# First attention of a two-layer block: value products in runs of three units, and a written TensorE order

## The chip, the cores and the metric

The kernel runs on one core of a Trainium2 chip. A core has TensorE (PE; its weight loads are listed as PEld), VectorE (DVE), ScalarE (ACT), GpSimd (POOL) and SyncE (SP), each with its own instruction queue, and 16 DMA engines that they share. The metric is device time of one launch in microseconds (us). Before the change it was 1098.98 us, the median of 3 runs (1098.36 to 1101.94).

## The reference

Two layers work on x of shape 4 x 1024 x 256 (batch, tokens, channels), all in float32. In each layer x is normalised and shifted, an attention is added to it with a gate, it is normalised again, and a mixture of experts is added with a gate. What matters here is the first layer:

```python
Q = (hidden_states @ Wq.T).reshape(b, t, h, d)            # h = 16 heads of d = 16
latent_k = hidden_states @ Wk_down.T                      # latent width l = 64
latent_v = hidden_states @ Wv_down.T
q_lat = jnp.einsum('bthd,hdl->bthl', Q, q_to_latent)
logits = jnp.einsum('bthl,bsl->bhts', q_lat, latent_k) / math.sqrt(l)
logits = jnp.where(causal[None, None], logits, jnp.float32(-1e+30))
attn = jax.nn.softmax(logits, axis=-1)
ctx_lat = jnp.einsum('bhts,bsl->bhtl', attn, latent_v)
heads = jnp.einsum('bhtl,hld->bthd', ctx_lat, v_up)
out = heads.reshape(b, t, h * d) @ Wout.T
```

Behind it each token goes to the 2 best of 16 experts, each of them two 256 x 256 products with a layer norm and a gelu in between. The second layer has a linear attention and a mixture of 8 experts with one choice.

## The kernel before

**Attention.** The 256 channels are two groups g of 8 heads, and the heads of a group are two sets o of four. For a batch b, a group g and a set o, the causal 1024 x 1024 logits of four heads are cut into nine *units* u (the table `UNITS`): each fills 512 columns for each of the four heads, some of them in two parts so that the causal triangle leaves no column empty. There are 4 x 2 x 2 x 9 = 144 units. `scores` (L388) makes one: for each head a product with a contraction over 32 rows, the four in four row groups of the array, into two PSUM tiles `ps_s` of two banks each (the pool `ps_s` has three). ACT takes the exponential of each half into `pT` (L396), and in the units that hold a piece of the diagonal POOL clears what lies above it (L399). The value products (`sums`, L453) take `pT` as the moving operand and 32 columns of `v` as the weights, the four heads in four column groups of the array, and add up over the units into one bank `ps_av` (the pool `ps_o` has one). Units 0, 1 and 2 end the first half of the queries and units 3 to 8 the second, and then `finish` turns and divides the sums on DVE (L411 to L416).

**Work in between.** The tasks in `k.around.tasks` are generators, cut into pieces by their `yield`. `prepare(b, g)` makes the next group's queries and keys: for g = 0 four transposing pieces (`ps_lnT`, L153) and four value projections (`ps_v`, L349), and for both g four query and key projections (`ps_qk`, L364). `project(b)` is the output projection, four pieces `ps_out` (L427). `experts0.rows(b)` normalises and routes the batch for the experts (`ps_lnT` L1057, `ps_route` L794, `ps_logits` L802), and `experts0.sort(hf)` ranks the tokens of batches 0 and 1 (hf = 0) or 2 and 3 (hf = 1) by expert (`ps_rank` L895, `ps_expert` L949, `ps_gain` L1138). All of them take their PSUM tiles from `misc`, an object of the class `Spread`; in this stage that is the one bank of `ps_m`.

**Riders.** At the end of `sort(hf)` a second kind of generator, `send`, is put on `k.around.riders`. Each of its 32 steps issues one scatter from POOL (L964, an indirect DMA of 128 rows) into the buffer `sorted`, from which the expert stage loads its tiles `xs` (L1008, on SP); a POOL load `hs<-rows_in` (L1165) goes ahead of each four, with three buffers. Each scatter is made to wait for the newest logits or expert product when it was written (`paced`, L964 and `k.anchor`). `Around.step(pieces, rides)` takes so many pieces and so many rider steps.

**The loop.** For unit n the loop adds the value products of all units up to n - 2, then makes the logits of n, then takes one piece of the tasks (two at every fourth unit of batches 1 and 2) and one rider step. At the end come the remaining value products, and one piece and two rider steps at a time until the last `project` is done.

**What sets the order.** POOL's instructions stand as the program writes them (`manual_schedule(engines={Pool})`); the order on PE, DVE, ACT and SP is that of a scheduler, which may put a piece in the middle of a unit's logits. Behind the attention come the experts (`Experts0.run`): `arrive` transposes four tiles of sorted rows (`ps_xT`, L1224), `hidden` is the first product (`ps_h`, L1247) and its statistics on DVE, `output` the second product (`ps_y`, L1312), while `rows(3)` and `sort(1)` run in between; the second half of the tiles waits for `sort(1)`'s 32 scatters.

Of the kernel before, what the change touches and what calls it, by code (L numbers as in the profile page):

```python
# [33 lines left out]
class Around:  # L34
# [9 lines left out]
    def step(self, pieces=1, rides=1):  # L44
        pieces -= self.over
        while pieces > 0 and self.tasks:
            done = next(self.tasks[0], None)
            if done is None:
                self.tasks.pop(0)
            else:  # L50
                pieces -= done
        self.over = max(-pieces, 0)
        for _ in range(rides):
            if self.riders and next(self.riders[0], self) is self:
                self.riders.pop(0)

    def finish_tasks(self):
        while self.tasks:
            self.step(rides=0)
# [191 lines left out]
def attention0(ctx, k, a, after_batch=lambda b: None):  # L251
# [23 lines left out]
    class Spread:  # L275


        early, turn = True, 0

        def tile(self, shape, dtype, tag=None, name=None):  # L280
            self.turn += 1
            if self.early and self.turn % 4:
                full = ps_s.tile([P, 2, 512], dtype, tag="s", name=name)[:, 0, :]
            else:
                full = ps_m.tile([P, 512], dtype, tag="m", name=name)
            size = 1
            for n in shape[1:]:
                size *= n
            full = full[: shape[0], :size]
            if len(shape) == 2:  # L290
                return full
            names = "abc"[: len(shape) - 1]
            return full.rearrange(
                f"p ({' '.join(names)}) -> p {' '.join(names)}", **dict(zip(names, shape[1:]))
            )

    misc = Spread()
# [43 lines left out]
    def prepare(b, g):  # L341

        if g == 0:
            yield from layer_norm_steps(k, b, hT, 0, misc, "m")
            for t in range(0, NT, 2):
                ps = misc.tile([P, 2, C], F32, name="ps_v")
                for i in range(2):
                    for cc in range(CC):
                        nc.tensor.matmul(  # L349
                            ps[:, i, :], lhsT=hT[:, cc, (t + i) * P : (t + i + 1) * P],  # L350
                            rhs=wv[:, cc, :], start=cc == 0, stop=cc == CC - 1,
                        )
                nc.scalar.copy(
                    vs[b % 2][:, t : t + 2, :, :D], ps.rearrange("p t (h d) -> p t h d", d=D)
                )
                yield 1
        else:
            gates[b] = spread_rows(k, work, 0, GATE, 0, "gate_a0", b, 1)[:, 0]
        qT, *kTs = qs[g]
        for w in (wq, wk):  # L360
            for hf in range(2):
                ps = misc.tile([P, 512], F32, name="ps_qk")
                for cc in range(CC):
                    nc.tensor.matmul(  # L364
                        ps, lhsT=w[:, cc, g * P : (g + 1) * P],
                        rhs=hT[:, cc, hf * 512 : (hf + 1) * 512],
                        start=cc == 0, stop=cc == CC - 1,
                    )
                cols = slice(hf * 512, (hf + 1) * 512)
                if w is wq:  # L370
                    nc.vector.tensor_copy(qT[:, cols], ps)  # L371
                else:
                    for o in range(2):
                        nc.vector.tensor_scalar(  # L374
                            kTs[o][:, cols], ps, par[:, o : o + 1], None, ALU.mult
                        )
                yield 1
        ready[b, g] = qT, kTs

    def scores(b, g, o, u):  # L380

        qT, kTs = ready[b, g]
        pair = [ps_s.tile([P, 2, 512], F32, tag="s", name="ps_s") for _ in range(2)]
        for kb, qc, c0, w, _ in UNITS[u]:
            q1 = (qc + 1) * 512
            for hh in range(4):
                rows = slice(32 * hh, 32 * hh + 32)
                k.anchor = nc.tensor.matmul(  # L388
                    pair[hh // 2][:, hh % 2, c0 : c0 + w],
                    lhsT=kTs[o][rows, kb * P : (kb + 1) * P], rhs=qT[rows, q1 - w : q1],  # L390
                    start=True, stop=True,
                ).ins
        pTs = []
        for ps in pair:
            pT = work.tile([P, 2, 512], F32, tag="pT", name="pT", bufs=7)
            nc.scalar.activation(pT, ps, AF.Exp, scale=1.0 / L**0.5)  # L396
            for _, _, c0, _, diagonal in UNITS[u]:
                if diagonal:
                    nc.gpsimd.affine_select(  # L399
                        out=pT[:, :, c0 : c0 + P], in_=pT[:, :, c0 : c0 + P],  # L400
                        compare_op=ALU.is_ge, fill=0.0, base=0,
                        pattern=[[0, 2], [1, P]], channel_multiplier=-1,
                    )
            pTs.append(pT)
        return pTs
# [33 lines left out]
    around = k.around.tasks  # L439

    def sums():

        for b in range(B):
            on = ons[b % 2]
            for g in range(2):
                for o in range(2):
                    for qc, pieces in enumerate(SUMS):
                        po = ps_o.tile([P, 512], F32, tag="o", name="ps_av")
                        for n, (u, i) in enumerate(pieces):
                            yield place[b, g, o, u]  # L450
                            kb, _, c0, w, _ = UNITS[u][i]
                            for hh in range(4):
                                nc.tensor.matmul(  # L453
                                    po[32 * hh : 32 * hh + 32, 512 - w :],
                                    lhsT=vs[b % 2][:, kb, 8 * g + 2 * hh + o, :],
                                    rhs=exps[b, g, o, u][hh // 2][:, hh % 2, c0 : c0 + w],
                                    start=n == 0, stop=n == len(pieces) - 1,
                                )
                        finish(b, g, o, qc, po, on)
            projects.append(project(b, on))  # L460
            around.append(projects[-1])
            after_batch(b)
# [3 lines left out]
    k.around.finish_tasks()  # L466
    setup_mod(k, 1, misc, mod)
    misc.early = False
    with k.tc.manual_schedule(engines={mybir.EngineType.Pool}):
        summing = sums()  # L470
        wanted = next(summing)
        for n, (b, g, o, u) in enumerate(units):
            if n == 8:
                k.clear_rows()
            if (o, u) == (0, 0):
                while (b, g) not in ready:
                    k.around.step(rides=0)
                coming = (b, 1) if g == 0 else (b + 1, 0)
                if coming[0] < B:
                    around.insert(0, prepare(*coming))  # L480
            while wanted is not None and wanted <= n - 2:
                wanted = next(summing, None)
            exps[b, g, o, u] = scores(b, g, o, u)
            k.around.step(2 if b in (1, 2) and n % 4 == 3 else 1)
        misc.early = True
        for _ in summing:
            pass
        while projects[-1] in around:
            k.around.step(rides=2)
# [1528 lines left out]
def two_layers(ctx: ExitStack, tc: tile.TileContext, a: dict, out: bass.AP):  # L2018
# [89 lines left out]

    load_x(0)
    again = stages(attention0, attention1, True)  # L2110


# [74 lines left out]
```

## Time and profile before

| what | value |
|---|---|
| time, median of 3 runs | 1098.98 us (1098.36 to 1101.94) |
| the profiled execution | 1087.63 us, of it 1085.8 us span from first to last instruction |
| PE busy, of the span | 945.7 us (87%) |
| ACT, DVE, POOL busy | 602.5, 620.4, 336.0 us |
| attention units, 45 to 507 us of the span | PE busy 451.81 us of the 467 us from 45 to 512 |
| logits L388, values L453, PE busy | 178.8 and 165.2 us |
| exponentials L396 on ACT | 288, 1022 ns each |
| scatters L964 on POOL | 96, 1002 ns each |

The page lists busy times by engine, the span in 40 slices, the chain of work that ended last, the groups of instructions, and DMA. A matmul of float32 shows as two records, so a unit's logits of four products are eight records, or sixteen where the unit has two parts. Line numbers are those of the kernel before; after the change the same code stands 9 to 27 lines lower.

### The profile page before, as it was taken

Reading aid. Unit: us, or ns where it says so; the run is one execution under the profiler, and the core shown is the slowest. Engines: PE = TensorE matmul, PEld = TensorE weight load, DVE = VectorE, ACT = ScalarE, POOL = GpSimd, SP = SyncE. Lnnn points to the kernel's source line nnn. Section 1 sums busy time; section 2 is a strip of 40 time slices with the busy share of each in tenths; the row PEclk is TensorE's granted clock in tenths of the full one; section 3 lists DMA queues with packets and bytes.
Section 4 is the critical chain, followed back from the end, with each engine's and each line's share of the span. In section 5 each row is a group of like instructions: output and inputs, shape, how many; then the busy total and the mean of one; then the engine's idle time right before and its main releaser. Section 6 shows DMA issues by size and latency. Waiting matters only on the chain.

```text
span 1085.8 us, 18090 instructions
## 1 busy us (share of the span) xinstructions
PE 945.7 (87%) x6072; PEld 559.8 (52%) x6072; DVE 620.4 (57%) x1987; ACT 602.5 (55%) x959; POOL 336.0 (31%) x528
## 2 busy tenths in 40 slices
PE   4899999999999999889679989986997989858760
PEld 2434434443443434335568878874464656547550
DVE  5822235422465155413676767993899968564572
ACT  0368655765477555775555657766654745523430
POOL 2013211311232234663004615612550100553632
PEclk9999999999999999999899999998999899989875
DMA  6995000100010001552825556624223201458764
GB/s 206 358 346 179 1 1 6 40 1 1 1 64 1 1 30 54 201 215 78 317 88 170 197 177 189 196 75 144 67 65 148 88 2 39 141 170 264 240 205 130
DMA packets 97142, 132.89 MB, mean 122 GB/s; under 512 B 8536, under 2 KB 84216, under 8 KB 96528
## 3 DMA queue, kind: packets, MB, share of 16 engines
q1 hardware_dynamic: 84656, 97.27, 26.9%
q0 software_dynamic: 11776, 33.57, 9.9%
q8 instruction: 52, 0.85, 0.3%
q10 hardware_dynamic: 608, 0.79, 0.3%
q14 instruction: 50, 0.41, 0.1%
HBM read 67.85 MB, written 63.75 MB: 121 GB/s over the span
## 4 chain that ended last, share of the span: by engine, by line
PE 63%; DVE 19%; issue 5%; DMA 5%; ACT 4%; POOL 1%; SPq 1%; DVEq 0%; ACTq 0%; POOLq 0%
PE ps_s L388 13%; PE ps_av L453 12%; PE ps_qk L364 6%; PE ps_y L1312 5%; PE ps_h L1247 4%; PE ps_v L349 3%; PE ps_out L427 3%; PE ps_pr L1609 3%; PE ps_y L1938 3%; PE ps_q L1537 2%; PE ps_k L1511 2%; DVE y L1601 2%; DMA ys<-results,index 2%; PE ps_lnT L1057 1%; DVE st L1258 1%
## 5 line engine op out<-in xcount | busy, mean ns | idle before, releaser
L396 ACT ACTIVATE pT<-ps_s 128x1024 f32<-128x1024 f32 x288 | 279.3, 1022 | 169.7 <-PE ps_s L388 167.2
L399 POOL TENSOR_SCALAR_AFFINE_SELECT pT<-pT 128x256 f32<-128x256 f32 x256 | 104.2, 431 | 328.4 <-ACT pT L396 323.7
L388 PE MATMUL ps_s<-qT,kT 32*128 32x512 f32 (+3 forms) x1536 | 178.8, 523 | 0.1
L453 PE MATMUL ps_av<-pT,v 128*32 128x512 f32 (+3 forms) x1536 | 165.2, 497 | 9.4 <-DVE turned L411 5.6
L964 POOL DMA_INDIRECT sorted<-hs,index x96 | 96.2, 1002 | 144.9 <-PE ps_y L1312 73.0
L974 POOL DMA_INDIRECT ys<-results,index x96 | 102.7, 1070 | 119.0 <-DMA results<-y 43.6
L388 PEld LDWEIGHTS ps_s<-qT,kT 32*128 32x128 f32 x1536 | 74.5, 185 | 95.5 <-issue 72.8
L453 PEld LDWEIGHTS ps_av<-pT,v 128*32 128x32 f32 x1536 | 40.6, 108 | 104.0 <-issue 58.7
L1247 PE MATMUL ps_h<-w,xT 128*128 x352 | 82.1, 386 | 6.5 <-DVE mv L1259 3.8
L1312 PE MATMUL ps_y<-w,act 128*128 x352 | 83.7, 392 | 4.2 <-DVE rs_seed L84 2.8
L411 DVE STREAM_TRANSPOSE turned<-ps_av 128x512 f32<-128x512 f32 x32 | 22.8, 712 | 98.9 <-PE ps_av L453 98.6
L1312 PEld LDWEIGHTS ps_y<-w,act 128*128 128x128 f32 x352 | 67.7, 197 | 14.0 <-ACT act L1295 4.8
L1247 PEld LDWEIGHTS ps_h<-w,xT 128*128 128x128 f32 x352 | 66.2, 193 | 15.9 <-issue 4.2
L1295 ACT ACTIVATE act<-ps_hT,gain 128x128 f32<-128x128 f32 x176 | 63.6, 463 | 16.9 <-PE ps_hT L1286 16.8
L1270 ACT ACTIVATE hid<-hid,nmr,rstd 128x256 f32<-128x256 f32 x88 | 47.5, 603 | 39.4 <-DVE nmr L1263 39.2
L1511 PE MATMUL ps_k<-wqkv,hT 128*128 128x512 f32 x128 | 61.9, 603 | 3.6 <-DMA wqkv<-in_wqkv_dram 2.8
L1938 PE MATMUL ps_y<-we,xT 128*128 x200 | 53.0, 412 | 10.6 <-ACT xT L1930 8.4
L371 DVE COPY qT<-ps_qk 128x512 f32<-128x512 f32 x16 | 11.0, 688 | 81.8 <-PE ps_qk L364 81.8
L103 DVE BATCH_NORM_STATS2 ln_st<-x 128x6 f32<-128x256 f32 x128 | 49.2, 407 | 0.5
L1255 DVE TENSOR_TENSOR hid<-ps_h,b 128x256 f32<-128x256 f32 x88 | 33.9, 415 | 26.6 <-PE ps_h L1247 21.5
L1938 PEld LDWEIGHTS ps_y<-we,xT 128*128 128x128 f32 x200 | 38.2, 204 | 20.1 <-ACT xT L1930 11.6
L374 DVE TENSOR_SCALAR kT<-ps_qk,par 128x512 f32<-128x512 f32 x32 | 22.5, 745 | 37.0 <-PE ps_qk L364 37.0
(223 smaller groups left out, 1499.4 us busy)
## 6 DMA issues: line engine op xcount, KB each, us to landing
xs<-sorted SPq DMA_DIRECT2D x69, 256.0 KB, 3.8
results<-y SPq DMA_DIRECT2D x69, 256.0 KB, 3.0
sorted<-zero SPq DMA_DIRECT2D x2, 6016.0 KB, 20.1
rows_in<-h SPq DMA_DIRECT2D x16, 512.0 KB, 2.9
hs<-rows_in POOLq DMA_DIRECT2D x32, 256.0 KB, 3.5
w<-in_w_dram SPq DMA_DIRECT2D x8, 1024.0 KB, 11.3
x<-in_x_dram SPq DMA_DIRECT2D x4, 1024.0 KB, 6.5
b<-in_b_dram SPq DMA_DIRECT2D x2, 2048.0 KB
```

The costliest lines, as they stand in the source:

```text
L364: nc.tensor.matmul(ps, lhsT=w[:, cc, g * P : (g + 1) * P], rhs=hT[:, cc, hf * 512 : (hf + 1) * 512], start=cc == 0, stop=cc == CC - 1,)
L388: k.anchor = nc.tensor.matmul(pair[hh // 2][:, hh % 2, c0 : c0 + w], lhsT=kTs[o][rows, kb * P : (kb + 1) * P], rhs=qT[rows, q1 - w : q1], ...
L396: nc.scalar.activation(pT, ps, AF.Exp, scale=1.0 / L**0.5)
L399: nc.gpsimd.affine_select(out=pT[:, :, c0 : c0 + P], in_=pT[:, :, c0 : c0 + P], compare_op=ALU.is_ge, fill=0.0, base=0, pattern=[[0, 2], [ ...
L453: nc.tensor.matmul(po[32 * hh : 32 * hh + 32, 512 - w :], lhsT=vs[b % 2][:, kb, 8 * g + 2 * hh + o, :], rhs=exps[b, g, o, u][hh // 2][:, h ...
L964: i = self.k.nc.gpsimd.indirect_dma_start(out=buffer.ap, out_offset=bass.IndirectOffsetOnAxis(ap=index, axis=0), in_=rows, in_offset=None, ...
L974: self.paced(self.k.nc.gpsimd.indirect_dma_start(out=rows, out_offset=None, in_=buffer.ap, in_offset=bass.IndirectOffsetOnAxis(ap=index, a ...
L1247: mm = nc.tensor.matmul(ph[:, j], lhsT=xTs[i // 2][:, j, cc], rhs=w1[:, cc, bass.ds(at[i + j], C)], start=cc == 0, stop=cc == CC - 1,)
L1295: o = nc.scalar.activation(act[:, j, cc], pt[:, j, cc], AF.Gelu, bias=gain[:, 1, cc, t : t + 1], scale=gain[:, 0, cc, t : t + 1],)
L1312: mm = nc.tensor.matmul(po[:, j], lhsT=acts[i // 2][:, j, cc], rhs=w2[:, cc, bass.ds(at[i + j], C)], start=cc == 0, stop=cc == CC - 1,)
L1511: k.anchor = nc.tensor.matmul(ps, lhsT=hT[:, cc, t * P : (t + 1) * P], rhs=wqkv[:, cc, C:], start=cc == 0, stop=cc == CC - 1,).ins
L1938: k.anchor = nc.tensor.matmul(po[:, j], lhsT=xT[:, j, cc], rhs=self.we[:, cc, bass.ds(at[j], C)], start=cc == 0, stop=cc == CC - 1,).ins
```

## The change

The class `Around` gets a method `piece` that takes one piece and tells its size. In the attention loop the order on PE, like that on POOL, is now the one that the program writes. Behind each unit's logits there comes either work of the tasks, or value products: while fewer than three units wait for their values, up to two small pieces or one large one (`ps_v`, `ps_qk`, `ps_out`) are taken; if none made a PSUM tile, the values are added, of up to three units in one run that ends at a multiple of three and holds no unit newer than the one before. After small pieces the next unit takes values, if there are any (`rest`). `Spread` gives the second tile of such a turn from the pool `ps_s` and the first from `ps_m`. Each unit takes one rider step as before (`step(0)`), and one more `step(1, 0)` stands behind the loop.

```diff
@@ class Around
+    def piece(self):
+
+        while self.tasks:
+            done = next(self.tasks[0], None)
+            if done is not None:
+                return done
+            self.tasks.pop(0)
+        return 0
@@ class Spread
-        early, turn = True, 0
+        early, turn, large = True, 0, 0
 
         def tile(self, shape, dtype, tag=None, name=None):
             self.turn += 1
-            if self.early and self.turn % 4:
+            self.large += name in ("ps_v", "ps_qk", "ps_out")
+            if self.turn % 4 if self.early else self.turn % 2 == 0:
                 full = ps_s.tile([P, 2, 512], dtype, tag="s", name=name)[:, 0, :]
             else:
                 full = ps_m.tile([P, 512], dtype, tag="m", name=name)
@@ attention0
     misc.early = False
-    with k.tc.manual_schedule(engines={mybir.EngineType.Pool}):
+    with k.tc.manual_schedule(engines={mybir.EngineType.Pool, mybir.EngineType.PE}):
         summing = sums()
-        wanted = next(summing)
+        wanted, rest = next(summing), False
         for n, (b, g, o, u) in enumerate(units):
...
-            while wanted is not None and wanted <= n - 2:
-                wanted = next(summing, None)
             exps[b, g, o, u] = scores(b, g, o, u)
-            k.around.step(2 if b in (1, 2) and n % 4 == 3 else 1)
+            misc.turn = misc.large = quiet = 0
+            while not rest and wanted > n - 3 and misc.turn < 2 and not misc.large:
+                done = misc.turn
+                quiet += k.around.piece()
+
+                if misc.turn == done and (done or quiet > 1 or not around):
+                    break
+            k.around.step(0)
+            if not misc.turn:
+
+                end = min(n if wanted != n - 2 else n - 1, wanted + 3 - wanted % 3)
+                while wanted is not None and wanted < end:
+                    wanted = next(summing, None)
+
+            rest = misc.turn and not misc.large and wanted < n
         misc.early = True
+        k.around.step(1, 0)
         for _ in summing:
             pass
```

## The prediction

> **What bounds the kernel now.** I read the page first, then the stretch of the attention, PE's timeline inside it, and the handover to the experts. Busy times, and the chain of work that ended last by engine:
>
> ```profile
> PE 945.7 (87%) x6072; PEld 559.8 (52%) x6072; DVE 620.4 (57%) x1987; ACT 602.5 (55%) x959; POOL 336.0 (31%) x528
> ...
> PE 63%; DVE 19%; issue 5%; DMA 5%; ACT 4%; POOL 1%; SPq 1%; DVEq 0%; ACTq 0%; POOLq 0%
> ```
>
> The windows view of the attention (stretch, its length, busy time of PE, PEld, DVE, ACT and POOL with instruction counts, granted clock) and of a stretch behind an idle PE:
>
> ```profile
> 45.00:512.00 467.00, 451.81 (x3612) 188.18 (x3613) 177.20 (x435) 295.67 (x319) 145.14 (x299) 0.99 0.23 78
> 842.10:848.20 6.10, 6.01 (x38) 4.87 (x39) 5.55 (x22) 6.10 (x12) 1.55 (x2) 0.51 0.44 136
> ```
>
> PE is the bound of the attention, with 15 of 467 us idle. So a change of its order pays only where it makes PE's own work cheaper, and costs only where PE must wait. PE's timeline (start, length to the modelled end, records):
>
> ```profile
> 169.43 1.13 PE L388 MATMUL ps_s<-qT,kT 32*128 32x512 f32 x4
> 170.49 1.99 PE L427 MATMUL ps_out<-wg,on 128*128 128x256 f32 x8
> 172.41 1.13 PE L388 MATMUL ps_s<-qT,kT 32*128 32x512 f32 x4
> 173.47 1.99 PE L427 MATMUL ps_out<-wg,on 128*128 128x256 f32 x8
> 175.40 1.50 PE L453 MATMUL ps_av<-pT,v 128*32 128x512 f32 x16
> 176.82 1.14 PE L388 MATMUL ps_s<-qT,kT 32*128 32x512 f32 x8
> 177.89 1.99 PE L427 MATMUL ps_out<-wg,on 128*128 128x256 f32 x8
> 179.82 1.06 PE L453 MATMUL ps_av<-pT,v 128*32 128x512 f32 x8
> 180.81 1.14 PE L388 MATMUL ps_s<-qT,kT 32*128 32x512 f32 x8
> ```
>
> From start to start, a unit's logits take 1.07 us, but so does half a unit when a piece is put in its middle (169.43 and 172.41: 1.06 each). Values of 512 columns take 0.99, of 768 columns 1.42: 0.43 per 256 columns and 0.135 per run. A large piece takes 1.93; in the long run of projections below, 15 products take 6.74, so four cost 1.80 and the change of shape 0.13. Now the handover:
>
> ```profile
> 494.62 1.22 POOL L964 DMA_INDIRECT sorted<-hs,index  x1 [0.30 <-PE ps_s L388]
> 497.39 6.84 SPq L1008 DMA_DIRECT2D xs<-sorted  x4
> 502.45 1.38 PE L388 MATMUL ps_s<-qT,kT 32*128 32x384 f32 x16
> 504.84 1.68 POOL L399 TENSOR_SCALAR_AFFINE_SELECT pT<-pT 128x256 f32<-128x256 f32 x4 [0.81 <-ACT pT L396]
> 507.20 6.74 PE L427 MATMUL ps_out<-wg,on 128*128 128x256 f32 x30
> 513.78 1.04 PE L1224 MATMUL ps_xT<-ident,xs 128*128 128x128 f32 x8
> 523.54 5.38 PE L1247 MATMUL ps_h<-w,xT 128*128 x16 [3.82 <-DVE mv L1259]
> ```
>
> All 32 scatters of the first sort are out at 494.62, eight us before the last unit's logits; the sorted rows are loaded under the attention, and the experts start without a gap. How fast scatters can go is seen in the second sort, and in the chain how the experts follow the last of them:
>
> ```profile
> 582.17 0.98 POOL L964 DMA_INDIRECT sorted<-hs,index  x1 [0.30 <-issue]
> 585.15 0.75 POOL L1165 DMA_DIRECT2D hs<-rows_in  x1 [0.73 <-DMA sorted<-hs,index]
> 627.49 0.98 POOL L964 DMA_INDIRECT sorted<-hs,index  x1 [0.30 <-PE ps_y L1312]
> ...
> 633.26 1.94 PE ps_xT L1224 x8
> ```
>
> **The change part by part.** I counted runs in the two built programs' order on PE.
>
> *Fewer runs.* Value runs (routing products, of the same shape, among them) go from 148 to 79: 69 x 0.135 = 9.3 us. Six units' logits were split by a piece and none is now: 6 x 1.05 = 6.3. Runs of full-array work go from 86 to 70: 16 x 0.13 = 2.1. Together 17.7 us, all on the bounding engine.
>
> *New waits on PE.* Key projections stand in neighbouring turns in six of the seven preparations in the loop, and the first tile of each turn is the single bank `ps_m`. The second must wait for two DVE copies of the first (745 ns each, L374, in the groups), 1.49 us and about 0.2 for the handovers, with only 1.07 of logits to hide them: 6 x 0.62 = 3.7. Before, a value run stood there too. A route product and the logits transpose behind it (L794, L802) now share a turn four times, and the rank's last two products once. The transpose waits for a 0.28 us copy on DVE and for what is queued there, the two 0.5 us operations of the next rows: between 0.5 and 1.8 each, I take 1.2, 5 x 1.2 = 6.0. Not waiting more: turns of about 2.07 us of PE work, less than the 2.38 us that a unit takes where exponentials set the pace (six units from 74.12 to 88.39), number 62 before and 50 now, short of it by 19.9 and 19.0 us in sum. Value runs of a triple always begin on a fresh `ps_av`, whose DVE turn is a unit old.
> So the attention gains 17.7 - 9.7 = 8 us; bounds 17.7 (nothing waits) and 0 (waits at 1.8, and every key projection behind a busy DVE).
>
> *The riders.* This is what the change moves without saying so. Small pieces now come only where fewer than three units wait, and large ones first, so `sort(0)` gets its last product, L1138, behind unit 127 instead of 107, and its 32 scatters start 20 units later, at one per unit. In POOL's order 16 stand between masks, 11 behind the last mask and ahead of the first `xs` load, 5 behind that load. The last unit's logits start at 502.45 - 8 = 494.5; its masks end 4.07 later as now (504.84 + 1.68), at 498.5. Eleven scatters at 1.28 and two `hs` loads at 1.05 put the last of them at 498.5 + 10 x 1.28 + 2.1 = 513.4. From a last scatter to the transposes of what was loaded it takes 633.26 - 627.49 = 5.8: `ps_xT` at 519.2, 5.4 us later than now. PE has nothing then: values 1.0 and 1.86, a route and its logits 0.7 and 16 projections 7.2 end near 506.3, and PE's written order holds the last batch's routing behind the first expert groups. Bounds for the 5.4: 0 (issue at 1.0) and 12 (each `hs` load waiting 3.3, as at 599.00).
>
> *What comes back.* Before, from 513.78 to 528.76, the second `ps_h` stood 3.82 us for a DVE that was at the last batch's residual and statistics. That work is 8 us earlier now and done. Against it, PE comes from 13 us of idling: behind a shorter idle the clock was granted at 0.51 for 6.1 us (842.10, above), and 5.38 against 3.46 us is what a `ps_h` group loses. With a cold first group (1.9 + 5.4) and a warm second (1.0 + 3.5, 0.5 of waits) the next routing piece is at 531.5, 2.7 later than 528.76. [...]
>
> *The five late scatters.* The first waits for the `xs` loads, the others for expert products; behind them on SP stand the later `xs` loads, the loads of w2 and the writes of `results`. First `ps_y` was at 542.19, 26 us behind w2's issue, and `xs` loads run two groups ahead: that covers them, 0; bound 5.
>
> *Sum.* +2.7 us where the routing of the last batch goes on; from there `sort(1)` and its scatters lead to 633.26 and the program is the same. The profiled execution is 1087.63 us (span 1085.8), 11.35 below the median of 1098.98; I add the difference to the median: 1101.7.
>
> **Rivals.** *The tail is cheaper than the gain.* If DVE is free when the new waits ask for it, the attention gains 17.7 and everything behind shifts by 9.7: 1092. For it: DVE is busy 177 of 467 us there. Against: it runs long queues just where routing pieces stand. It decides from a gain of 14 us.
> *Scatters go slower than their best.* An `hs` load waits until its buffer's four scatters have landed; at 599.00 that took 3.3 us. Twice that adds 6.6: 1108. For it: of the five loads from 585 to 616 in the second sort three waited, 0.7 to 3.3; against: two did not, and the 1.3 us between scatters holds. It decides from 1 us of wait for each.
> *The new order does nothing for PE.* If PE waits for exponentials and masks wherever three units are held back (seven `pT` buffers, eight wanted), the gain is 0 and the start of the experts goes with it: 1110. Against: turns with a large piece take 3 us of PE against 2.04 of ACT.
>
> **How the numbers follow.** A measurement can tell 0.3%, 3.3 us. The likeliest case, 0.45, has its own range 1096 to 1107 and lies within 0.3% in 0.28, slower in 0.15, faster in 0.02. The cheap tail has 0.22 (faster), slow scatters 0.22 and no gain 0.11 (slower). Faster 0.24, same 0.28, slower 0.48. The range leaves out the outer part of the first and of the last two.
>
> **What would show it.** Value groups of L453 with some 28 records behind one start; no logits group of four records; last `ps_av` some 8 us earlier than 505.70; scatters still issued after it; a gap of 10 to 15 us on PE ahead of the first `ps_xT`, ended by the `xs` load, that starts later than 513.78; a low granted clock behind it; the first scatter of the second sort (576.66) later by about 3. It is wrong if the experts start without a gap, or if the rank of the second sort comes earlier than 565.

## The result, and the profile after

The changed kernel takes 1105.59 us (median, 1100.29 to 1110.16); before, on the same chip, 1098.66 (1090.70 to 1103.83). The ratio is 1.0071, 95% interval 1.0053 to 1.0089: 6.9 us slower. The range held it; the single number, 1101.7, meant a loss of 2.7 us. The profiled execution of the changed kernel is 1101.17 us (span 1099.4), 4.4 below its median, while that of before was 11 below its own. So the two profiles stand 13.6 us apart where the medians stand 6.9 apart. The profiled execution of before (1087.63) is faster than all 20 timed ones; it lies where the set of `b_late` below, whose kernel before is faster throughout, has it (1083.48 to 1090.40), and the record doesn't say on which chip it was taken. Milestones below are compared within the profiles, sizes of effects by ratios of the sets.

Busy times and the chain of work that ended last, of the changed kernel:

```profile
PE 937.9 (85%) x6072; PEld 564.5 (51%) x6072; DVE 615.6 (56%) x1987; ACT 604.5 (55%) x959; POOL 333.4 (30%) x528
...
PE 65%; DVE 14%; DMA 8%; issue 5%; ACT 5%; POOL 1%; SPq 1%; DVEq 0%; ACTq 0%; POOLq 0%
```

PE works 7.8 us less and the program ends later: the time went into PE's waits, and DMA's share of the chain rose from 5% to 8%. Windows of the changed kernel (columns as in the prediction; clock third from the end):

```profile
45.00:512.00 467.00, 445.18 (x3628) 194.53 (x3628) 177.44 (x446) 297.06 (x319) 128.02 (x284) 0.97 0.21 71
400.00:512.00 112.00, 102.36 (x854) 47.31 (x854) 55.01 (x155) 64.10 (x71) 48.77 (x82) 0.94 0.32 115
512.00:560.00 48.00, 24.05 (x129) 20.29 (x130) 21.48 (x92) 19.29 (x38) 11.24 (x13) 0.75 0.68 242
```

In the attention PE stands 22 us in place of 15, and the clock is granted at 0.97 in place of 0.99, all of that lost in six stretches of 3.41 or 6.83 us at 0.50. In the 48 us behind it PE is busy for 24 us (before 37.47). Line numbers are now those of the changed kernel. PE's timeline shows the new order and one of its waits:

```profile
188.63 1.99 PE L438 MATMUL ps_out<-wg,on 128*128 128x256 f32 x8
190.55 1.14 PE L399 MATMUL ps_s<-qT,kT 32*128 32x512 f32 x8
191.62 2.36 PE L464 MATMUL ps_av<-pT,v 128*32 128x512 f32 x32
193.91 1.14 PE L399 MATMUL ps_s<-qT,kT 32*128 32x512 f32 x8
197.92 2.36 PE L464 MATMUL ps_av<-pT,v 128*32 128x512 f32 x12 [2.86 <-DVE turned L422]
```

Values of three units in one run, no unit's logits split, and then a value run that waits 2.86 us for the one `ps_av`, because DVE has not yet transposed it. The handover to the experts, from the timelines of POOL, SP and PE:

```profile
504.08 0.99 POOL L991 DMA_INDIRECT sorted<-hs,index  x1 [0.16 <-issue]
...
508.74 0.76 POOL L1192 DMA_DIRECT2D hs<-rows_in  x1 [1.10 <-DMA sorted<-hs,index]
...
519.59 0.97 POOL L991 DMA_INDIRECT sorted<-hs,index  x1 [0.31 <-issue]
...
522.15 2.26 SPq L1035 DMA_DIRECT2D xs<-sorted  x4
...
525.27 1.94 PE L1251 MATMUL ps_xT<-ident,xs 128*128 128x128 f32 x8 [13.43 <-DMA xs<-sorted]
```

The 27th scatter is out at 519.59, the `xs` loads follow, and PE idles for 13.43 us. The first `ps_xT` starts 11.5 us later than before (513.78). The trace shows a second place, which the prediction had put down at nothing, the last five scatters. From the timelines, and then from the chain of work that ended last (start, length, what):

```profile
538.51 1.01 POOL L991 DMA_INDIRECT sorted<-hs,index  x1 [3.01 <-PE ps_xT L1251]
554.80 0.97 POOL L991 DMA_INDIRECT sorted<-hs,index  x1 [15.28 <-PE ps_xT L1251]
...
545.15 13.00 SPq L1035 DMA_DIRECT2D xs<-sorted  x4
...
543.19 0.60 PE L1084 MATMUL ps_lnT<-ident,h 128*128 128x128 f32 x4
553.46 1.94 PE L1251 MATMUL ps_xT<-ident,xs 128*128 128x128 f32 x8 [9.66 <-DMA xs<-sorted]
```

```profile
524.05 3.81 DMA xs<-sorted
...
528.64 5.54 DMA sorted<-hs,index
...
534.72 2.95 DMA xs<-sorted
...
538.51 6.58 DMA sorted<-hs,index
...
545.15 8.17 DMA xs<-sorted
```

Late scatters and `xs` loads of the same buffer wait for each other in turn: the chain goes from a load to a scatter to the next load and back, and PE stands 9.66 us for such a load. Of the five scatters (from 528.64 to 562.73) the trace puts the waits of four down to `xs` loads or to the `ps_xT` products that read them; the fifth follows 0.3 us behind the fourth.

The order has a second consequence, which is not one of time. The four `xs` loads at 522.15 bring the first eight tiles and wait only for the scatters written ahead of them in the program, the last of them at 519.59. Five scatters are written, and run, behind them (528.64 to 562.73): the rows that these bring for those tiles arrive after the tiles were read. So the changed kernel does not do quite the work of the one before, and its order would have to be repaired before use. `b_late`, `a_dve` and `a_scalar` below have the same five behind; the kernel before, and the runs with two rider steps, have all 32 ahead.

**A ledger of the attention.** For every 2 us window between 47 and 501 us I take PE's idle time, and busy time x (1 - granted clock) as clock loss. Before: 15.11 idle and 3.23 clock loss, 18.3. After: 20.96 and 11.06, 32.0. (The 20.5 and 10.9 in the recorded expectations left out the stretch from 399 to 400.) From the first logits to the last the stretch went from 458.5 us (45.1 to 503.6) to 454.8 (46.2 to 501.0), 3.7 less. So the work itself shrank by 3.7 + 13.7 = 17.4 us, and 13.7 came back as waits and low clock.

### The profile page after: what moved, and what is told of

Same layout as the page of the kernel before. It is cut to its first block, busy times and chain, and to the rows that moved or that the text cites. A ratio compares the mean times of both kernels' runs of the same rounds, so it can differ in the third digit from the quotient of the medians.

```text
span 1099.4 us, 18085 instructions
## 1 busy us (share of the span) xinstructions
PE 937.9 (85%) x6072; PEld 564.5 (51%) x6072; DVE 615.6 (56%) x1987; ACT 604.5 (55%) x959; POOL 333.4 (30%) x528
## 4 chain that ended last, share of the span: by engine, by line
PE 65%; DVE 14%; DMA 8%; issue 5%; ACT 5%; POOL 1%; SPq 1%; DVEq 0%; ACTq 0%; POOLq 0%
PE ps_s L399 14%; PE ps_av L464 12%; PE ps_qk L375 5%; PE ps_y L1339 5%; PE ps_h L1274 5%; PE ps_v L360 3%; PE ps_pr L1636 3%; DMA xs<-sorted 2%; PE ps_k L1538 2%; PE ps_q L1564 2%; PE ps_y L1965 2%; PE ps_out L438 2%; DMA ys<-results,index 2%; DMA sorted<-hs,index 2%; PE ps_hT L1313 1%
## 5 line engine op out<-in xcount | busy, mean ns | idle before, releaser
L410 POOL TENSOR_SCALAR_AFFINE_SELECT pT<-pT 128x256 f32<-128x256 f32 x256 | 101.5, 416 | 363.5 <-ACT pT L407 357.4
L399 PE MATMUL ps_s<-qT,kT 32*128 32x512 f32 (+3 forms) x1536 | 184.5, 531 | 1.5 <-ACT pT L407 0.5
L464 PE MATMUL ps_av<-pT,v 128*32 128x512 f32 (+3 forms) x1536 | 147.3, 507 | 7.0 <-DVE turned L422 7.0
L464 PEld LDWEIGHTS ps_av<-pT,v 128*32 128x32 f32 x1536 | 43.8, 111 | 109.0 <-issue 77.0
L1339 PEld LDWEIGHTS ps_y<-w,act 128*128 128x128 f32 x352 | 67.9, 198 | 13.6 <-ACT act L1322 4.5
L1322 ACT ACTIVATE act<-ps_hT,gain 128x128 f32<-128x128 f32 x176 | 63.7, 463 | 17.1 <-PE ps_hT L1313 15.1
L1965 PE MATMUL ps_y<-we,xT 128*128 x200 | 52.3, 406 | 13.7 <-ACT xT L1957 5.6
L1251 PE MATMUL ps_xT<-ident,xs 128*128 128x128 f32 x176 | 26.1, 294 | 26.1 <-DMA xs<-sorted 24.6
L1348 DVE TENSOR_TENSOR y<-ps_y,b 128x256 f32<-128x256 f32 x88 | 35.3, 418 | 20.8 <-PE ps_y L1339 20.0
```

What stands on the lines that cost most here:

```text
L399: k.anchor = nc.tensor.matmul(pair[hh // 2][:, hh % 2, c0 : c0 + w], lhsT=kTs[o][rows, kb * P : (kb + 1) * P], rhs=qT[rows, q1 - w : q1], ...
L410: nc.gpsimd.affine_select(out=pT[:, :, c0 : c0 + P], in_=pT[:, :, c0 : c0 + P], compare_op=ALU.is_ge, fill=0.0, base=0, pattern=[[0, 2], [ ...
L464: nc.tensor.matmul(po[32 * hh : 32 * hh + 32, 512 - w :], lhsT=vs[b % 2][:, kb, 8 * g + 2 * hh + o, :], rhs=exps[b, g, o, u][hh // 2][:, h ...
L1322: o = nc.scalar.activation(act[:, j, cc], pt[:, j, cc], AF.Gelu, bias=gain[:, 1, cc, t : t + 1], scale=gain[:, 0, cc, t : t + 1],)
L1339: mm = nc.tensor.matmul(po[:, j], lhsT=acts[i // 2][:, j, cc], rhs=w2[:, cc, bass.ds(at[i + j], C)], start=cc == 0, stop=cc == CC - 1,)
L1965: k.anchor = nc.tensor.matmul(po[:, j], lhsT=xT[:, j, cc], rhs=self.we[:, cc, bass.ds(at[j], C)], start=cc == 0, stop=cc == CC - 1,).ins
```

## The experiments

Labels that begin with b are made from the kernel before, with a from the changed one. All ratios are to the kernel before, timed on the same chip in the same set. The sets come from two chips: the kernel before has a median of 1087.6 or 1085.6 us in those of experiments 1 to 4, 7 and `a_dve`, and of 1098.0 or 1099.0 in those of 5, 8 and `a_scalar`. The changed kernel itself was timed only for the result, so wherever a ratio is set against its 1.0071, it is assumed that the change costs the same share in every set. Two theories stood at the start: A, the late scatters cost the time; B, new waits of PE inside the attention do.

**1. The tail without the gain (`b_late`).**

```diff
-            k.around.step(2 if b in (1, 2) and n % 4 == 3 else 1)
+            k.around.step(2 if b in (1, 2) and n % 4 == 3 else 1, int(n > 126))
```

> The kernel before, all its orders of PE, DVE and ACT as they were, but the riders (the 32 scatters of the first sort and their hs loads) are held until the loop is behind unit 126, where the changed kernel has them. It has the cost of the changed kernel without its gain. Theory A (the late scatters are what made the change slower): the first ps_xT goes from 513.78 to about 527, PE stands 13 to 15 us ahead of it, and the time is 10 to 14 us above before. Theory B (the late scatters cost no more than the 5.4 us of my prediction, and the gain was lost to new waits of PE inside the attention): first ps_xT below 520, 0 to 5 us above before.

Measured 1.0187 (1.0164 to 1.0210), 20 us. POOL's and PE's timelines:

```profile
470.91 1.07 POOL L964 DMA_INDIRECT sorted<-hs,index  x1 [6.78 <-DMA hs<-rows_in]
...
530.75 1.94 PE L1224 MATMUL ps_xT<-ident,xs 128*128 128x128 f32 x8 [12.70 <-DMA xs<-sorted]
```

The gap of 12.7 us is the one of the changed kernel, and A holds in kind. The size is above both theories, and not all of it is the tail: the first scatter waits 6.78 us for its `hs` load with a mask behind it, and PE stands 8 us for that mask, which the changed kernel doesn't.

**2. Both kernels without the scatters (`b_noscat`, `a_noscat`).**

```diff
-                    self.sorting.scatter(hs[:, i], k.sorted0[hf], index[:, s, t + i : t + i + 1])
+                    if hf:
+                        self.sorting.scatter(hs[:, i], k.sorted0[hf], index[:, s, t + i : t + i + 1])
```

> The kernel before, without the 32 scatters of the first sort (left out of the computation: the first experts get cleared rows); the hs loads and all orders of PE, DVE and ACT stay. Both theories: the scatters of the kernel before lie under the attention, so first ps_xT stays within 2 us of 513.78 and the time within 3 us of before. If it is over 5 us faster, scatters cost something along the way (POOL late with its masks), which neither theory has.

> The changed kernel without the 32 scatters of the first sort (left out of the computation: the first experts get cleared rows); the hs loads and all orders of PE, DVE and ACT stay. This is the change without its tail. Theory A: first ps_xT some 2 to 3 us earlier than before (511, where values end at 504.4 and 16 projections follow), no idle PE ahead of it, and a time 2 to 6 us below before. Theory B: still 2 to 7 us above before.

Measured 0.9956 (0.9939 to 0.9973) and 0.9940 (0.9922 to 0.9957). The window from 400 to 512 us, first of `b_noscat`, then of `a_noscat`:

```profile
400.00:512.00 112.00, 108.78 (x929) 50.18 (x922) 45.75 (x120) 71.88 (x79) 31.20 (x72) 1.00 0.30 108
```

```profile
400.00:512.00 112.00, 102.46 (x858) 47.86 (x854) 54.66 (x153) 64.57 (x71) 28.79 (x63) 0.94 0.28 100
```

Three things follow. Scatters cost the changed kernel 1.0071 - 0.9940 (ratios of two sets), some 14 us, and the kernel before only 4.8: A. They do cost the kernel before something, against both theories: without them its last value product starts at 500.0 in place of 507.0. And without scatters the two kernels are within 0.2% of each other, so the change as such is worth next to nothing at the end: B too. In this window the changed order idles 9.5 us without scatters and 9.6 with them, and runs at 0.94 in both; the old one, without them, idles 3.2 us and runs at 1.00.

**3. The scatters earlier (`a_rides2`).** Two steps behind each unit put all 32 ahead of the last masks.

```diff
-            k.around.step(0)
+            k.around.step(0, 2)
```

> The changed kernel with two steps of the riders behind each unit in place of one, so that all 32 scatters stand ahead of the last masks in POOL's order. Theory A with POOL to spare: the last scatter is out near 500, PE's gap ahead of the first ps_xT shrinks from 13.4 to under 5 us, and the time is 4 to 8 us below the changed kernel (within 2 us of before). Rival C: POOL has no room for 2 x 1.28 us beside masks in a unit of 2.4 us, the masks of the last 16 units come late, values wait for them, and the time is no better than the changed kernel's, with PE's waits inside the attention instead of behind it.

Measured 1.0096 (1.0077 to 1.0115): rival C's outcome, no better than the changed kernel. From POOL's and PE's timelines:

```profile
504.28 0.76 POOL L1192 DMA_DIRECT2D hs<-rows_in  x1 [5.34 <-DMA sorted<-hs,index]
...
516.25 0.75 POOL L1192 DMA_DIRECT2D hs<-rows_in  x1 [5.40 <-DMA sorted<-hs,index]
517.01 1.48 POOL L410 TENSOR_SCALAR_AFFINE_SELECT pT<-pT 128x256 f32<-128x256 f32 x4
...
508.11 2.28 PE L464 MATMUL ps_av<-pT,v 128*32 128x512 f32 x8 [5.70 <-POOL pT L410]
517.49 2.62 PE L464 MATMUL ps_av<-pT,v 128*32 128x384 f32 x16 [7.10 <-POOL pT L410]
```

But the reason that C gave, the scatters' 1.28 us, isn't what these lines show. The masks stand behind `hs` loads that wait for a buffer, that is for a scatter to land; experiment 5 tests it.

**4. The first sort's loads moved to SP (`a_sp2`, `b_sp`).**

```diff
-            k.nc.gpsimd.dma_start(hs, k.rows_in[HB * hf + b].part([i, i + 1]))
+            (k.nc.gpsimd if hf else k.nc.sync).dma_start(hs, k.rows_in[HB * hf + b].part([i, i + 1]))
```

> The changed kernel with two steps of the riders behind each unit, as in the run with two steps, and with the first sort's hs loads issued by SP in place of POOL, so that POOL's masks no longer stand behind a load that waits for scatters to land (5.34, 5.40 and 2.52 us there). Theory F (those waits, not the scatters' own 1.28 us, hold the masks back): last masks near 504 instead of 518, first ps_xT 513 to 517 instead of 527.6, and the time 8 to 12 us below the changed kernel, 0.995 to 1.001 of before. Rival: the scatters' own time is what the masks wait for, and the last masks stay at 512 or later, first ps_xT above 520.

> The kernel before with the first sort's hs loads issued by SP in place of POOL. Without the scatters it was 0.9956 of before, its attention 7 us shorter. Theory F (the hs loads that wait on POOL for scatters to land, 4.33, 1.56 and 2.00 us, are what the masks were held back by): 0.995 to 0.998 of before, first ps_xT near 508. Rival: the scatters themselves, 1.28 us each between the masks, cost that time: within 2 us of before, 0.998 to 1.002.

Measured 1.0087 (1.0062 to 1.0112) for `a_sp2`, whose last masks ended at 515.6, and 1.0052 (1.0032 to 1.0071) for `b_sp`, slower than either theory had it. Theory F fell, and the trace of `b_sp` says why. POOL still has waiting `hs` loads there:

```profile
477.81 0.77 POOL L1165 DMA_DIRECT2D hs<-rows_in  x1 [6.15 <-DMA sorted<-hs,index]
...
489.54 0.76 POOL L1165 DMA_DIRECT2D hs<-rows_in  x1 [3.31 <-DMA sorted<-hs,index]
```

In the built programs' order these loads read the rows of batch 2. They belong to the *second* sort, wanted some 80 us later; the scheduler put them between the first sort's scatters and masks, where they wait for buffers. The kernel before has the same three, at 476.69, 486.62 and 497.83. This gave theory G, that these three loads are what holds the masks back.

**5. The three loads kept behind the last mask (`b_keep`, and `a_keep2` with two steps).**

```diff
@@ scores
-                    nc.gpsimd.affine_select(
+                    k.mask = nc.gpsimd.affine_select(
...
-                    )
+                    ).ins
@@ send
-            k.nc.gpsimd.dma_start(hs, k.rows_in[HB * hf + b].part([i, i + 1]))
+            i = k.nc.gpsimd.dma_start(hs, k.rows_in[HB * hf + b].part([i, i + 1])).ins
+            if hf:
+                k.tc.add_manual_dep(
+                    i, k.mask.name,
+                    mybir.DependencyInfo(mybir.DependencyClass.NoSync, mybir.DependencyReason.DATA),
+                    reason="behind the last mask",
+                )
```

> The kernel before with one thing changed: three hs loads of the second sort (rows of batch 2, wanted some 80 us later), which the scheduler put between the scatters and masks of the attention's end in POOL's order (476.69, 486.62 and 497.83 of before, waiting 4.33, 1.56 and 2.00 us there), are kept behind the last mask. PE, DVE and ACT keep their orders. Theory G (these three loads hold the masks back, and with them the values): PE's waits of 2.24 and 1.58 us at 476.9 and 484.2 go, first ps_xT is at 507 to 510 in place of 513.8, and the time is 0.995 to 0.998 of before, most of what leaving out all scatters gave (0.9956). Rival (the scatters' own 1.28 us between the masks are what costs): within 0.999 to 1.002 of before.

> The changed kernel with two steps of the riders behind each unit, and the second sort's hs loads kept behind the last mask. Theory G: the waits of 5.34 and 5.40 us ahead of the last masks go, the last masks end by 508 in place of 519, first ps_xT is at 514 to 519, and the time 0.998 to 1.004 of before, against 1.0096 for two steps alone and 0.994 without scatters. Rival (32 scatters of 1.28 us in the last 17 units are too many beside the masks, wherever the loads stand): first ps_xT at 521 or later, 1.005 of before or more.

Both came out as G had them, but for the first `ps_xT` of `b_keep` at 510.64, just behind its range: `b_keep` 0.9970 (0.9949 to 0.9992), `a_keep2` 0.9982 (0.9960 to 1.0004). (Behind the edit their line numbers are six higher.) In the kernel before, POOL and then PE:

```profile
476.69 0.76 POOL L1165 DMA_DIRECT2D hs<-rows_in  x1 [4.33 <-DMA sorted<-hs,index]
...
480.03 0.78 POOL L399 TENSOR_SCALAR_AFFINE_SELECT pT<-pT 128x256 f32<-128x256 f32 x2
...
480.51 1.41 PE L453 MATMUL ps_av<-pT,v 128*32 128x512 f32 x8 [2.24 <-POOL pT L399]
```

and in `b_keep`, where PE's timeline shows no wait for a mask from 470 us to the last values:

```profile
501.70 1.68 POOL L399 TENSOR_SCALAR_AFFINE_SELECT pT<-pT 128x256 f32<-128x256 f32 x4 [0.81 <-ACT pT L396]
503.32 2.25 POOL L1165 DMA_DIRECT2D hs<-rows_in  x3
...
510.64 1.04 PE L1230 MATMUL ps_xT<-ident,xs 128*128 128x128 f32 x8
```

In `a_keep2` PE's wait ahead of the experts is almost gone:

```profile
508.93 7.07 PE L438 MATMUL ps_out<-wg,on 128*128 128x256 f32 x32
516.60 0.63 PE L1257 MATMUL ps_xT<-ident,xs 128*128 128x128 f32 x4 [0.60 <-DMA xs<-sorted]
```

So two rider steps and the moved loads together take the changed kernel from 1.0071 to 0.9982, some 10 us over two sets, without touching the change in the attention, and they put all scatters ahead of the loads again. It is then level with the kernel before. `b_keep` needs only the moved loads, is faster than the kernel before, and is within its interval of what leaving out the scatters gave.

**6. DVE's order (`a_dve`) and DVE's load (`a_scalar`).** These two aimed at theory B's waits. The first has DVE in written order, the second makes the normalised rows of batches 0 to 2 on ACT.

```diff
-    with k.tc.manual_schedule(engines={mybir.EngineType.Pool, mybir.EngineType.PE}):
+    with k.tc.manual_schedule(engines={mybir.EngineType.Pool, mybir.EngineType.PE, mybir.EngineType.DVE}):
```

```diff
-            k.around.tasks.append(experts0.rows(b, b == B - 1))
+            k.around.tasks.append(experts0.rows(b, True))
```

> The changed kernel with DVE's order in the attention's loop as written too; the orders of PE and POOL are the same. Between 47 and 500 us the changed kernel has 20.5 us of idle PE and 10.9 us lost to a low granted clock (2 us windows, busy time by 1 minus clock); the kernel before has 15.1 and 3.3. Theory D (PE waits for ps_av transposes that stand behind row statistics on DVE, 2.86 and 4.10 us, and for the routing's copy, 2.53 us, and each wait is followed by some 4 us at half clock): with the transposes ahead of the next rows' work the two long waits fall below 1 us, idle and clock loss together fall from 31 to 20 to 24, the last values go from 504.4 to 494 to 499, and the time is 4 to 9 us below the changed kernel, 0.998 to 1.003 of before. Rival E (the waits are only moved: a copy or a residual that PE needs now stands behind another one): within 3 us of the changed kernel, 1.005 to 1.010 of before.

> The changed kernel with the normalised rows of batches 0 to 2 made on ACT and two wide DVE operations (as the kernel already does for batch 3) in place of eight DVE operations for four tiles: DVE's queue ahead of the ps_av transposes is 1.8 us shorter for each four tiles (2 x 1.23 against 8 x 0.54), ACT's is 2.4 us longer; PE and POOL keep their orders. Theory D again, in a form that leaves the rest of DVE's order to the scheduler: PE's waits of 2.86 (193.9) and 4.10 us (470.0) shrink to 2 or less, idle PE and clock loss between 47 and 500 us go from 31 to 23 to 27, and the time is 2 to 5 us below the changed kernel, 1.002 to 1.006 of before. Rival E: other waits take their place (exponentials behind ACT's rows, a route's copy behind the wide operations), idle and clock loss stay at 29 or more, and the time within 2 us of the changed kernel.

Measured 1.0251 (1.0228 to 1.0273) and 1.0126 (1.0098 to 1.0155), both slower than D and E had them. PE in `a_dve`, and in `a_scalar`:

```profile
198.04 0.48 PE L1084 MATMUL ps_lnT<-ident,h 128*128 128x128 f32 x1 [3.60 <-DVE h L1064]
```

```profile
204.35 1.94 PE L1084 MATMUL ps_lnT<-ident,h 128*128 128x128 f32 x8 [4.35 <-DVE h L1073]
```

In `a_scalar` the two long waits for `ps_av` shrink from 2.86 and 4.10 to 0.83 and 1.20 us: DVE's work on the next rows is what the transposes stood behind. But the rows then arrive 4.35 us late at their own transposes on PE, twice. In `a_dve` the rows' work follows the transposes, and PE waits 3.60 and 3.44 us for it instead, and 4.63 for DVE in the sort. Idle and clock loss between 47 and 501 us rise to 45.5 in `a_dve` and 38.5 in `a_scalar`. That is theory E in kind, though it had the times within 3 us of the changed kernel: in PE's fixed order the wait is moved, not removed. Both versions lose at the end as well, since their scatters start later still (457.9 and 454.8 against 448.8).

**7. The written order alone (`b_written`).**

```diff
-    with k.tc.manual_schedule(engines={mybir.EngineType.Pool}):
+    with k.tc.manual_schedule(engines={mybir.EngineType.Pool, mybir.EngineType.PE}):
```

> The kernel before with PE's order in the attention's loop as written, as the changed kernel has it, instead of the scheduler's. If the written order by itself makes PE wait (a piece is no longer moved to where its input is ready), idle PE between 47 and 500 us grows by 5 us or more and the time is 1.005 or more of before. If the loss of the changed kernel lies in its new neighbours (pieces and values gathered, quiet DVE work ahead of values) and not in the written order, it stays within 0.997 to 1.004.

Measured 1.0058 (1.0035 to 1.0081): the written order alone costs the kernel before 6.3 us. Idle PE between 47 and 501 us goes from 15.1 to 25.7.

```profile
169.23 1.98 PE L364 MATMUL ps_qk<-hT,wk 128*128 128x512 f32 x4
172.72 0.48 PE L427 MATMUL ps_out<-wg,on 128*128 128x256 f32 x1 [1.50 <-DVE kT L374]
```

Two pieces that share the single bank `ps_m` stand side by side in the written order; the scheduler had a value run or logits between them. The changed kernel was written for a fixed order and has only 0.43 us in its worst such places, so this is a cost of the fixed order that it mostly avoids.

**8. All remedies at once (`a_best`).** `a_keep2` with the first sort's loads on SP as well.

> The changed kernel with two steps of the riders behind each unit, the second sort's hs loads behind the last mask, and the first sort's eight hs loads issued by SP in place of POOL (about 1.06 us of POOL each). Theory G: what is left in the run before (two PE waits of 2.05 us near 498 and 501 for masks that stand behind scatters, last masks at 505.9, first ps_xT at 516.6, 0.998 of before) shrinks with POOL's shorter queue: last masks near 504, first ps_xT at 512 to 515, and 0.994 to 0.998 of before; without scatters it was 0.994. Rival: SP's queue, where the loads now wait for scatters ahead of the rows of batch 2 and the experts' weights, makes the experts start later: first ps_xT at 518 or later, 1.000 of before or more.

Measured 1.0012 (0.9990 to 1.0034), the rival's outcome in time: first `ps_xT` at 518.85. The place is PE's timeline at a routing's logits:

```profile
489.65 0.64 PE L821 MATMUL ps_route<-hT,wr 128*32 128x128 f32 x16
496.65 0.44 PE L829 MATMUL ps_logits<-ident,turned 128*128 128x128 f32 x1 [6.36 <-DVE turned L826]
```

That wait is 2.53 us in the changed kernel. DVE's copy stood there for 3.47 us behind something that the trace doesn't name and that isn't DVE's. SP's stores of the rows of batch 2 now stand behind four `hs` loads that are spread over 23.9 us of SP's queue, which would explain it; it was not tried apart.

## Why the prediction came out as it did

The range and the direction of most chance were right, and so was the mechanism (a gain in the attention, a scatter tail that eats it). Two terms of the sum were wrong, both too good: the attention's gain, put at 8 us, was 2.6 to 3.7 (inside its bounds), and the five late scatters, put at 0 with a bound of 5, cost 6.9. By the traces the loss was 13.6 us and not 2.7. That the medians stand only 6.9 apart kept the time in the range, and this is partly luck: 13.6 us on top of 1098.66 would have been 1112, outside 1096 to 1107, the range of the case held likeliest.

- **Fewer runs**, 17.7 us: the ledger has 17.4. Right.
- **New waits on PE**, 9.7 us: 5.9 more of idle time than before. Inside that sum, key projections wait 0.43 us each for the single bank where 0.62 was predicted; route to logits 4.5 us in four places, predicted 6.0. The sentence that failed is "Value runs of a triple always begin on a fresh `ps_av`, whose DVE turn is a unit old". Twice DVE was in the statistics and rows of the next batch, and the transposes came 2.86 and 4.10 us late (`a_scalar` shows this cause). In sum it cost little more than before, though: the kernel before waits for `ps_av` transposes four times, 5.6 us together and 3.19 at most, the changed one 7.0. And it was offset by something that the prediction hadn't seen either: before had waits of 2.24 and 1.58 us for masks, which went with the scatters.
- **The clock in the attention**, not priced at all: 7.8 us more of clock loss. I weighed the low clock only for the handover. It turned the predicted 8 us of gain into 3.7 by the logits' own start, 2.6 by their end. This is the larger error of the two within the attention, since idle time alone was overestimated.
- **The riders**: PE's idle time was predicted at 13, and is 13.43. The 27th scatter is 6.2 us later than predicted (519.59 against 513.4), 5.4 of that because the attention ended later than predicted, the rest about one `hs` load's wait (1.10). From the scatter to `ps_xT` 5.7 us, predicted 5.8. Right, with the attention's error passed on.
- **What comes back**, 2.7 us: `ps_xT` starts 11.5 us late, the next routing piece 8.1 (536.86 against 528.76), so 3.4 came back. The second `ps_h` waits 0.78 in place of 3.82. Right.
- **The five late scatters**, "that covers them, 0; bound 5": wrong, and the step that failed by most. I asked only whether the `xs` loads are issued early enough, not that late scatters and early loads of one buffer wait for each other in turn. The routing pieces behind them show the price: 7.6 us late at 543.19 (before 535.55), 14.5 late at 562.20 (before 547.69), so 6.9.
- **Sum**: the first scatter of the second sort comes 12.4 us late (589.10 against 576.66) where 3 were predicted; at the last product of these experts (`ps_y`, 748.3 and 759.6) the traces stand 11.3 apart, and at the end 13.6, the last 2.3 in code that the change doesn't touch. By medians it is 6.9. Where the other 4 to 7 us go, and why single executions of before, from 1090.7 to 1103.8, differ by as much as that, was not studied and stays open.

Of the rivals, "scatters go slower than their best" took place for its named reason, but in the kernel before, in `a_rides2` and among the last five, not in the tail's first part, where one load waited 1.10 us.

What else stays open: no run removes the changed kernel's waits on DVE inside the attention without new ones, so the cost of its low clock is read from windows and not shown by an experiment. Whether the five late scatters alone would give back their 6.9 us wasn't tried: `a_keep2` moves them together with the tail.

## What to carry to other kernels

Where an order is rewritten, follow each queue that rides on it to its last element, and ask of every transfer behind the boundary who waits for it and for whom it waits: here five late scatters and the `xs` loads of one buffer waited in turn, at a price of 6.9 us, and the loads at 522.15, which the program writes ahead of those scatters, didn't wait for them at all. A load that waits for a buffer can hold up the work queued behind it: in `a_rides2` POOL's last masks started at 517.01, behind an `hs` load that had waited 5.40 us. So look in the built order for prefetches that a scheduler has put ahead of work that is due. On a tightly packed PE a short wait should be priced with the low clock that may follow it: here 7.8 us more of clock loss came with 5.9 us more of idle time.

## What the runs showed of the chip that was not expected

The granted clock fell behind some short waits of PE and not behind others. Between 45 and 505 us it was 0.50 in six stretches of the changed kernel's profile, five of 3.41 us (from 54.42, 197.78, 296.77, 443.54 and 491.33) and one of 6.83 (from 474.26), and in two of the kernel before, of 3.41 us each (from 52.78 and 438.48); in the rest it was 1.00. The changed kernel around its waits of 1.62, 4.10 and 2.53 us, and then `b_sp` around waits of 3.14 us (from 478.54) and 3.34 us (from 487.45):

```profile
293.36:296.77 3.41, 1.79 (x31) 0.92 (x32) 0.29 (x1) 2.23 (x3) 0.81 (x2) 1.00 0.00 0
296.77:300.18 3.41, 3.41 (x24) 1.03 (x20) 0.00 (x0) 1.94 (x2) 1.49 (x4) 0.50 0.00 0
...
470.85:474.26 3.41, 0.30 (x12) 0.11 (x4) 3.24 (x9) 1.94 (x2) 1.94 (x5) 1.00 0.11 38
474.26:477.67 3.41, 2.42 (x12) 0.75 (x16) 3.35 (x9) 0.00 (x0) 1.47 (x2) 0.50 0.32 108
477.67:481.09 3.42, 3.42 (x36) 1.39 (x28) 0.48 (x1) 1.79 (x2) 0.69 (x2) 0.50 0.24 84
481.09:484.50 3.41, 3.23 (x22) 1.62 (x24) 0.00 (x0) 2.36 (x4) 2.81 (x6) 1.00 0.13 43
...
487.92:491.33 3.41, 0.92 (x7) 0.74 (x9) 2.49 (x7) 0.27 (x1) 0.65 (x1) 1.00 0.20 72
491.33:494.74 3.41, 3.41 (x20) 0.60 (x16) 0.00 (x0) 0.00 (x0) 1.61 (x2) 0.50 1.02 298
```

```profile
477.00:479.00 2.00, 1.54 (x20) 1.08 (x16) 0.00 (x0) 1.81 (x3) 0.88 (x2) 1.00 1.03 420
479.00:481.00 2.00, 0.00 (x0) 0.00 (x0) 0.00 (x0) 1.40 (x2) 1.70 (x2) 1.00 1.12 465
481.00:483.00 2.00, 1.32 (x8) 0.29 (x8) 0.00 (x0) 0.00 (x0) 1.83 (x4) 1.00 0.98 408
483.00:485.00 2.00, 2.00 (x22) 0.87 (x22) 0.00 (x0) 0.75 (x1) 1.83 (x6) 1.00 1.00 406
...
487.00:489.00 2.00, 0.45 (x4) 0.00 (x0) 0.00 (x0) 1.50 (x2) 0.00 (x0) 1.00 0.08 29
489.00:491.00 2.00, 0.21 (x2) 0.19 (x4) 0.00 (x0) 0.00 (x0) 1.28 (x3) 0.83 0.00 0
491.00:493.00 2.00, 2.00 (x8) 0.36 (x8) 0.00 (x0) 0.00 (x0) 2.00 (x5) 0.50 0.67 201
```

In these rows the length of a wait doesn't tell whether the clock falls: it fell behind 1.62 us in the changed kernel and stayed at 1.00 behind 3.14 in `b_sp`. In the 3.41 us ahead of its six falls the changed kernel's PE was idle for 2.58, 2.72, 1.62, 0.77, 3.11 and 2.49 us, in order of time; that of the kernel before for 3.12 and 2.81 ahead of its two, and for 1.58 between 486.27 and 489.69, with the clock at 1.00 behind it. Behind the wait of 4.10 us the low clock lasted 6.83 us; PE was busy for 2.42 us of the first half of it and for all of the second. What decides between a fall and none isn't shown by these runs.

The second thing is how long an `hs` load waited for a buffer: up to 7.33 us in `a_sp2`, where a scatter took 3.1 us from issue to landing in the median. In the stretch from 500 to 520 us of `a_rides2`, with its waits of 5.4 us, the DMA engines were 84% busy at 330 GB/s.
